# A four-layer graph network on one core: the pair factor of the hyperbolic layers as a degree-4 polynomial, with the old program behind a run-time guard

## The chip, the core and the metric

The kernel runs on one core of one Trainium2 chip. A core has five engines that run their own instruction streams: PE (matrix products, with its weight loads listed as PEld), DVE (VectorE), ACT (ScalarE, activation functions by tables that are loaded as sets), POOL (GpSimd) and SP (SyncE, which issues most DMAs here). SBUF is the on-chip memory with 128 partitions, PSUM the memory that PE writes its products to. The metric is device time in microseconds (us) from one launch of the whole program, the median of several runs. The profile beside it is one execution taken by the hardware profiler.

## What is computed

There are N = 3327 nodes with D = 64 features, and one adjacency matrix `adj` of zeros and ones (density 0.0048). Four layers follow one another. Each takes `h = relu(layernorm(x))` and adds its result to `x`.

```python
h = max(layernorm(x), 0); x = x + L0(h, adj)     # hyperbolic attention
h = max(layernorm(x), 0); x = x + L1(h, adj)     # decayed neighbour sum: w @ (h @ weight) + bias
h = max(layernorm(x), 0); x = x + L2(h, adj)     # signed attention and two GRUs, times the diagonal of adj
h = max(layernorm(x), 0); x = x + L3(h, adj)     # hyperbolic attention with curvature c = 1 / r^2

# L0 and L3
x_t  = logmap0(h)                                 # h * artanh(|h|) / |h|
att  = sigmoid(left(x_t)[:, None] + right(x_t)[None, :] + b) * adj
sup  = sum over j of att[i, j] * logmap(h_i, h_j) # a vector for each pair of nodes
out  = proj(expmap(h, sup))
```

`logmap(h_i, h_j)` holds `artanh(|s|) s / |s|`, where `s` is the Moebius sum of `-h_i` and `h_j`. So each pair of nodes has a direction that is linear in `h_j` and a scalar factor that is not.

## The kernel before

The host pads the nodes to NP = 3328 = 26 x 128, that is by **one** row of zeros in `x`, and one row and one column of zeros in `adj`, which is given transposed (`adjT`). The tile `X` [128, 26, 64] holds all nodes for the whole program; node `t * 128 + p` lies in partition `p`, slot `t`, so the padding row is partition 127 of slot 25. The four layers run one after another: `hyperbolic(att0, ...)`, `decay_sum()`, `signed_gat()`, `hyperbolic(att3, ...)`, and then `X` is written to `out`. Which instruction goes to which engine is written in the code; the order within an engine, buffers and waits are set by the framework's scheduler, except that in the pair loop of `hyperbolic` the order on ACT is kept as written (`manual_schedule`), because tables are switched there by hand.

`hyperbolic` has three parts.

1. A set-up: layer norm and relu into `H`, the squared norms `x2`, the logarithmic map for the attention terms, and transpositions by PE (`to_columns`) into `LdT`, `L2T` and `RT`, whose rows are the 64 features and two more.
2. The pair loop: over 4 chunks of W = 832 target columns and 13 pairs of source blocks of 128 rows. A pair loads 832 KB of `adjT`, makes two sigmoids and multiplies them into `adj` on POOL. For each of the two blocks PE makes `den` (line 274) and `dd` (line 276) in two halves of 416 columns, DVE clips and combines them (277, 278), POOL multiplies (282), ACT takes Ln, Exp and Square (284 to 287), POOL and DVE make a Newton step (288, 289), DVE forms `z` and `v` (292 to 295), ACT takes two logarithms after another table load (303, 304), DVE corrects for rounding (305, 306), POOL adds (307, 308), DVE multiplies up to the weight `w` (309, 311), and PE sums `rows^T w` over the 26 blocks in PSUM (`acc`, 313).
3. An ending on [128, 26, 64] tiles: Moebius algebra on DVE, node by node, and `X += res`.

`decay_sum` and `signed_gat` also go over blocks of `adjT`. In `decay_sum`, the sum comes out transposed, as `outT` [64, NP], and is written for all NP columns by

```python
A.activation(outT[:, c0 + h * BK:c0 + (h + 1) * BK], acc[h], AF.Identity, bias=bias)
```

after which `X` gets `outT` transposed, all 26 slots of it. In `signed_gat`, `X` gets the layer's result times `dcol`, the diagonal of `adjT`.

Of the kernel before, what the change touches and what calls it, by code (L numbers as in the profile page):

```python
# [9 lines left out]
F32 = mybir.dt.float32  # L10
BF = mybir.dt.bfloat16
AF = mybir.ActivationFunctionType
OP = mybir.AluOpType
# [3 lines left out]
N = 3327          # nodes  # L17
P = 128
T = 26            # node tiles
NP = T * P        # nodes, padded with rows and columns of zeros  # L20
D = 64
BK = 416          # columns of one PSUM bank in use; 8 of them make NP
# [4 lines left out]


@with_exitstack
def tile_gnn4(ctx: ExitStack, tc: tile.TileContext, x, adjT, att0, b0, w1, bias1, w_gat, a_gat,  # L30
              wih_e, whh_e, bih_e, bhh_e, wih_n, whh_n, bih_n, bhh_n, r3, att3, b3, out):
    """x [NP, D]; adjT [NP, NP] with adjT[j, i] = adj[i, j]; the GRU weights come as [in, 3D],
    their biases as [D, 3]. Node n = t * P + p lies in partition p, slot t."""
# [18 lines left out]
    tiny_c = column(1e-19, "tiny_c")  # L52

    X = const.tile([P, T, D], F32, name="X")
    nc.sync.dma_start(X, x.rearrange("(t p) d -> p t d", p=P))
# [5 lines left out]
    def wide(t, n=D):  # L61
        """[P, T] -> [P, T, n], the same value along the last dim."""
        return t[:, :, None].to_broadcast([P, T, n])

    def bcast_rows(dram, n=1):
        """A DRAM vector of n values in every partition."""
        return bass.AP(tensor=dram.tensor, offset=dram.offset, ap=[[0, P], [1, n]])

    def sqrt_(pool, src, name):
        """sqrt of a small positive tile: the table's value and one Newton step."""  # L70
        s0 = pool.tile(list(src.shape), F32, name=name)
        rc = pool.tile(list(src.shape), F32, name=name + "_r")
        A.activation(s0, src, AF.Sqrt)
        V.reciprocal(rc, s0)
        V.tensor_mul(rc, rc, src)
        V.tensor_add(s0, s0, rc)
        V.tensor_scalar(s0, s0, 0.5, None, op0=OP.mult)
        return s0

    def norm_relu(pool, h):  # L80
        """h = max(layernorm(X), 0)"""
# [14 lines left out]
    def to_columns(psum, dst, src, rows, post=None):  # L96
        """dst [rows, NP] = src [P, T, rows] transposed"""
# [7 lines left out]
    def to_rows(psum, src, rows, use):  # L105
        """use(t0, n, [P, n, rows]) for src [rows, NP] transposed, some tiles at a time"""
# [9 lines left out]
    def split3(pool, src, name):  # L116
        """fp32 src as the exact sum of three bf16 tiles"""
# [11 lines left out]
    def drop_diagonal(a, b, c0, w):  # L129
        """a [P, w] holds adjT[b*P:, c0:c0+w]: zero what lies on the diagonal"""  # L130
# [4 lines left out]

    def hyperbolic(att, b_att, r, min_norm, min_norm2):
        """X += proj(expmap(h, sum_j sigmoid(left + right) adj logmap(h_i, h_j))).

        In coordinates scaled by sqrt(c) the ball has radius 1. With den = 1 - 2xy + x2 y2 and
        d2 = |x - y|^2, |num|^2 = den d2 holds for num = -(1 - 2xy + y2) x + (1 - x2) y, so that  # L140
        the summand is att artanh(|num|/den) num/|num|. num is linear in (y, y2, 1): the sum over j
        is one product with those rows. The summand of j = i is zero."""
        W = 2 * BK
        with ExitStack() as st:
            pers = st.enter_context(tc.tile_pool(name="hy", bufs=1))
            rows = pers.tile([P, T, D + 2], F32, name="rows")      # [h', x2', 1]
# [9 lines left out]
            lns = pers.tile([P, 1], F32, name="lns")      # brings den d2 into the range of Ln  # L156
# [5 lines left out]
            with tc.tile_pool(name="hyp", bufs=1) as tp, tc.tile_pool(name="hyps", bufs=2, space=PSUM) as ps:  # L162
# [40 lines left out]
                rows2 = tp.tile([P, T, D + 2], F32, name="rows2")  # [h', 1, x2']  # L203
# [4 lines left out]
                # x_t = h artanh(z)/z with z = |h'|; below the floor artanh(z)/z is 1 in fp32  # L208
# [25 lines left out]
                V.tensor_scalar(RT, LdT, sc, None, op0=OP.mult)    # [-2h', x2', 1]  # L234
# [11 lines left out]
            with tc.tile_pool(name="hyadj", bufs=3) as ap, tc.tile_pool(name="hyw", bufs=2) as wk, \  # L246
# [3 lines left out]
                for c in range(NP // W):  # L250
                    c0 = c * W
                    acc = [pa.tile([D + 2, BK], F32, name=f"acc{h}") for h in range(2)]
                    for b2 in range(T // 2):
# [12 lines left out]
                        for s in range(2):  # L266
# [13 lines left out]
                            # y = -2/|num|, by logarithms and one Newton step  # L280
# [9 lines left out]
                            # z = |num|/den, clipped  # L290
# [6 lines left out]
                        A.preload_act_table_set("natural_log")  # the set with the more exact Ln  # L297
                        for s, (y, z, v) in enumerate(pair):
                            b = 2 * b2 + s
                            # lu = 2 artanh(z), with what was rounded off in 1 + z and 1 - z  # L300
# [17 lines left out]
            with tc.tile_pool(name="hye", bufs=1) as tp, tc.tile_pool(name="hyps", bufs=2, space=PSUM) as ps:  # L318
# [3 lines left out]
                m, q, s = M[:, :, :D], M[:, :, D], M[:, :, D + 1]  # L322

                def dot(a, b_, name):
                    prod = tp.tile([P, T, D], F32, name="prod", bufs=2)
                    V.tensor_mul(prod, a, b_)
                    o = tp.tile([P, T], F32, name=name)
                    V.reduce_sum(o, prod, axis=AX.X)
                    return o

                def axpby(a, xx, b_, yy, name):
                    """a x + b y, a and b one value per node"""
                    o = tp.tile([P, T, D], F32, name=name)
                    o2 = tp.tile([P, T, D], F32, name="prod", bufs=2)
                    V.tensor_mul(o, xx, wide(a))
                    V.tensor_mul(o2, yy, wide(b_))
                    V.tensor_add(o, o, o2)
                    return o

                # v = sum_j w (-(1 - 2xy + y2) x + (1 - x2) y)  # L340
                ca = dot(hs, m, "ca")
                V.scalar_tensor_tensor(ca, ca, 2.0, s, op0=OP.mult, op1=OP.subtract)
                V.tensor_sub(ca, ca, q)
                bx = tp.tile([P, T], F32, name="bx")
                V.tensor_scalar(bx, x2, -1.0, 1.0, op0=OP.mult, op1=OP.add)
                vv = axpby(ca, hs, bx, m, "vv")
                f = tp.tile([P, T], F32, name="f")
                V.tensor_scalar(f, bx, MIN_NORM, None, op0=OP.max)
                th = tp.tile([P, T], F32, name="th")
                if r is None:  # L350
                    # expmap of h at the point f v: second = h tanh(t)/(t g), t = |h|/g,
                    # g = max(1 - |f v|^2, MIN_NORM); below 1e-4 tanh(t)/t is 1 in fp32
                    V.tensor_mul(vv, vv, wide(f))
                    p2 = dot(vv, vv, "p2")
                    by = tp.tile([P, T], F32, name="by")
                    V.tensor_scalar(by, p2, -1.0, 1.0, op0=OP.mult, op1=OP.add)
                    g = tp.tile([P, T], F32, name="g")
                    V.tensor_scalar(g, by, MIN_NORM, None, op0=OP.max)
                    V.reciprocal(g, g)
                    t = tp.tile([P, T], F32, name="t")  # L360
                    V.tensor_scalar(t, x2, min_norm2, None, op0=OP.max)
                    t = sqrt_(tp, t, "ts")
                    V.tensor_mul(t, t, g)
                    V.tensor_scalar(t, t, 1e-4, None, op0=OP.max)
                    A.activation(th, t, AF.Tanh)
                    V.reciprocal(t, t)
                    V.tensor_mul(th, th, t)
                    V.tensor_mul(th, th, g)
                    second = tp.tile([P, T, D], F32, name="second")
                    V.tensor_mul(second, hs, wide(th))  # L370
                    point, p2, bp = vv, p2, by
                else:
                    # expmap of f v at the point h': second = v tanh(t)/t, t = max(|v|, min_norm/f)
                    t = dot(vv, vv, "t")
                    V.tensor_scalar(t, t, 1e-8, None, op0=OP.max)
                    t = sqrt_(tp, t, "ts")
                    V.reciprocal(f, f)
                    V.scalar_tensor_tensor(t, f, um, t, op0=OP.mult, op1=OP.max)
                    A.activation(th, t, AF.Tanh)
                    V.reciprocal(t, t)  # L380
                    V.tensor_mul(th, th, t)
                    V.tensor_mul(vv, vv, wide(th))
                    point, second, p2, bp = hs, vv, x2, bx
                # mobius_add(point, second)
                y2 = dot(second, second, "y2")
                xy = dot(point, second, "xy")
                V.tensor_scalar(xy, xy, 2.0, 1.0, op0=OP.mult, op1=OP.add)
                a1 = tp.tile([P, T], F32, name="a1")
                V.tensor_add(a1, xy, y2)
                res = axpby(a1, point, bp, second, "res")  # L390
                V.tensor_mul(y2, y2, p2)
                V.tensor_add(y2, y2, xy)
                V.tensor_scalar(y2, y2, MIN_NORM, None, op0=OP.max)
                V.reciprocal(y2, y2)
                V.tensor_mul(res, res, wide(y2))
                # proj
                n2 = dot(res, res, "n2")
                V.tensor_scalar(n2, n2, maxn2, None, op0=OP.max)
                n2 = sqrt_(tp, n2, "ns")
                V.reciprocal(n2, n2)  # L400
                V.tensor_scalar(n2, n2, 1.0 - 0.004, 1.0, op0=OP.mult, op1=OP.min)
                if isqc is not None:
                    V.tensor_scalar(n2, n2, isqc, None, op0=OP.mult)
# [283 lines left out]
```

## Time and profile before

| what | value |
|---|---|
| median of 3 runs | 4569.69 us (4567.25 to 4571.99) |
| profiled execution: span from first to last instruction | 4563.9 us |
| profiled execution: own time | not listed apart from the span |
| instructions | 22255 |
| PE, PEld, DVE, ACT, POOL busy | 2499.5, 1044.7, 3750.4, 2000.1, 2514.0 us |
| HBM read, written | 178.41 MB, 0.85 MB |
| mean granted TensorE clock | 0.621 of full |
| `X` loaded; last write of `X`; DMA of `out` issued | 0.8 us; 4555.8 us; 4557.7 us |

Lines of a group read: line of the kernel, engine, operation, tile written <- tiles read, shape, how often | busy us in all, mean ns of one | idle time of the engine just before them and what ended it. Rows of a stretch read: start and end, length, and the busy time of PE, PEld, DVE, ACT and POOL with the number of instructions, then the granted clock of PE (1.00 is full), the mean busy share of the 16 DMA engines and GB/s.

### The profile page before, as it was taken

What the parts mean: (1) busy time and instruction counts of PE and PEld (TensorE: products, weight loads), DVE (VectorE), ACT (ScalarE), POOL (GpSimd) and SP (SyncE); (2) the same over time, 40 slices, a digit from 0 to 9 for tenths busy, and PEclk for the clock granted to TensorE, in tenths of its full rate; (3) what the DMA queues carried; (4) which work ended last, traced back from release to release, by engine and by line L of the source; (5) the groups of instructions that cost most, each with busy time, mean ns of one, the idle gap of its engine ahead of it and who ended that gap; (6) DMA issues with size and microseconds to landing.
All of it is one profiled execution on the core that took longest, in us unless ns stands there. A gap on an engine that the chain in (4) does not pass through costs nothing.

```text
span 4563.9 us, 22255 instructions
## 1 busy us (share of the span) xinstructions
PE 2499.5 (55%) x6796; PEld 1044.7 (23%) x6796; DVE 3750.4 (82%) x3373; ACT 2000.1 (44%) x2106; POOL 2514.0 (55%) x1077
## 2 busy tenths in 40 slices
PE   6555455445454452566899686555455544545541
PEld 3111111111111110233576123111111111111110
DVE  6999899989989998654544646999899989989998
ACT  3444444444444443233565224444444454444442
POOL 3676666666666664466000004676666666666672
PEclk7555555555555555799999555555555555555555
DMA  1000000000000000343453000000000000000000
GB/s 38 23 30 23 23 30 23 30 23 30 23 30 23 23 30 0 135 150 105 134 153 107 0 0 30 30 23 30 22 23 30 30 23 22 30 23 22 30 23 8
DMA packets 63144, 180.70 MB, mean 40 GB/s; under 512 B 16112, under 2 KB 16432, under 8 KB 63024
## 3 DMA queue, kind: packets, MB, share of 16 engines
q1 hardware_dynamic: 58544, 179.26, 12.6%
q8 instruction: 53, 0.87, 0.1%
q10 hardware_dynamic: 4480, 0.02, 0.1%
q14 instruction: 67, 0.55, 0.0%
HBM read 178.41 MB, written 0.85 MB: 39 GB/s over the span
## 4 chain that ended last, share of the span: by engine, by line
DVE 67%; PE 14%; POOL 13%; issue 3%; ACT 2%; DMA 0%; POOLq 0%; ACTq 0%; DVEq 0%; SPq 0%
DVE lu L309 12%; DVE v L305 12%; DVE z L292 10%; POOL lu L308 10%; DVE w L311 6%; DVE v L306 6%; DVE y L289 4%; DVE z L293 3%; PE pv L562 3%; DVE dm L277 3%; DVE df L278 2%; POOL S L476 2%; PE pn L559 2%; DVE v L295 2%; PE acc L468 1%
## 5 line engine op out<-in xcount | busy, mean ns | idle before, releaser
L313 PE MATMUL acc<-w,rows 128*66 128x416 f32 x832 | 624.5, 905 | 887.4 <-DVE w L311 887.4
L276 PE MATMUL dd<-RT,L2T 66*128 66x416 f32 x832 | 660.8, 895 | 787.2 <-DVE df L278 787.2
L309 DVE TENSOR_TENSOR lu<-lu,y 128x832 f32<-128x832 f32 x208 | 564.5, 2714 | 219.9 <-POOL lu L308 219.9
L308 POOL TENSOR_TENSOR lu<-lu,v 128x832 f32<-128x832 f32 x208 | 458.1, 2203 | 452.9 <-DVE v L306 452.9
L282 POOL TENSOR_TENSOR p<-dm,df 128x832 f32<-128x832 f32 x208 | 463.5, 2228 | 378.2 <-DVE df L278 378.2
L305 DVE SCALAR_TENSOR_TENSOR v<-z,v 128x832 f32<-128x832 f32 x208 | 635.0, 3053 | 0.0
L307 POOL TENSOR_TENSOR lu<-lu,lv 128x832 f32<-128x832 f32 x208 | 404.7, 1946 | 410.2 <-ACT lv L304 335.0
L288 POOL TENSOR_TENSOR q<-q,p 128x832 f32<-128x832 f32 x208 | 546.0, 2625 | 150.9 <-ACT q L287 150.9
L303 ACT ACTIVATE lu<-z,one_c 128x832 f32<-128x832 f32 x208 | 205.6, 988 | 858.4 <-DVE z L293 858.4
L284 ACT ACTIVATE y<-p,tiny_c,lns 128x832 f32<-128x832 f32 x208 | 224.7, 1080 | 790.9 <-DVE lu L309 774.4
L274 PE MATMUL den<-RT,LdT 66*128 66x416 f32 x832 | 507.3, 738 | 53.7 <-DVE dm L277 52.8
L276 PEld LDWEIGHTS dd<-RT,L2T 66*128 66x128 f32 x832 | 217.2, 303 | 1212.4 <-DVE df L278 1122.7
L292 DVE TENSOR_TENSOR z<-df,y 128x832 f32<-128x832 f32 x208 | 478.0, 2298 | 2.8
L264 POOL TENSOR_TENSOR adj<-adj,sig 128x1664 f32<-128x1664 f32 x104 | 422.0, 4057 | 76.9 <-ACT sig L261 76.8
L313 PEld LDWEIGHTS acc<-w,rows 128*66 128x66 f32 x832 | 158.2, 220 | 1303.6 <-DVE w L311 1062.1
L311 DVE SCALAR_TENSOR_TENSOR w<-lu,adj 128x832 f32<-128x832 f32 x208 | 331.4, 1593 | 0.3
L274 PEld LDWEIGHTS den<-RT,LdT 66*128 66x128 f32 x832 | 226.7, 281 | 335.1 <-issue 189.8
L306 DVE SCALAR_TENSOR_TENSOR v<-z,v 128x832 f32<-128x832 f32 x208 | 294.6, 1416 | 0.0
L278 DVE SCALAR_TENSOR_TENSOR df<-dm,floor,dd 128x416 f32<-128x416 f32 x416 | 264.8, 636 | 6.3 <-PE dd L276 6.3
L562 PE MATMUL pv<-value,H 128*64 128x416 f32 x832 | 268.0, 512 | 0.0
L289 DVE SCALAR_TENSOR_TENSOR y<-q,y 128x832 f32<-128x832 f32 x208 | 211.8, 1018 | 67.6 <-POOL q L288 67.6
L548 DVE TENSOR_SCALAR mask<-adj 128x832 bf16<-128x832 f32 x208 | 124.4, 600 | 155.2 <-PE pc L561 138.6
(300 smaller groups left out, 4284.0 us busy)
## 6 DMA issues: line engine op xcount, KB each, us to landing
adj<-in SPq DMA_DIRECT2D x156, 832.0 KB, 4.5
adj<-in SPq DMA_DIRECT2D x104, 416.0 KB, 3.3
X<-in SPq DMA_DIRECT2D x1, 832.0 KB, 7.7
out<-X SPq DMA_DIRECT2D x1, 832.0 KB, 5.3
wie<-in SPq DMA_DIRECT2D x1, 96.0 KB, 2.1
whe<-in SPq DMA_DIRECT2D x1, 48.0 KB, 2.3
win<-in SPq DMA_DIRECT2D x1, 48.0 KB, 2.3
whn<-in SPq DMA_DIRECT2D x1, 48.0 KB, 2.2
```

What stands on the lines that cost most here:

```text
L264: G.tensor_tensor(adj, adj, sig, op=OP.mult)
L274: PE.matmul(den, LdT[:, b * P:(b + 1) * P], RT[:, cs], start=True, stop=True)
L276: PE.matmul(dd, L2T[:, b * P:(b + 1) * P], RT[:, cs], start=True, stop=True)
L282: G.tensor_tensor(p, dm, df, op=OP.mult)
L288: G.tensor_tensor(q, q, p, op=OP.mult)
L292: V.tensor_mul(z, df, y)
L305: V.scalar_tensor_tensor(v, z, 1.0, v, op0=OP.add, op1=OP.subtract)
L306: V.scalar_tensor_tensor(v, z, 2.0, v, op0=OP.mult, op1=OP.subtract)
L308: G.tensor_tensor(lu, lu, v, op=OP.add)
L309: V.tensor_mul(lu, lu, y)
L311: V.scalar_tensor_tensor(w, lu, -0.25, adj[:, s, :], op0=OP.mult, op1=OP.mult)
L313: PE.matmul(acc[h], rows[:, b, :], w[:, h * BK:(h + 1) * BK], start=(b == 0), stop=(b == T - 1))
```

## The change

Both hyperbolic layers get a new function, `hyperbolic_series`. It takes one product per pair of nodes, L = LT^T RT, and replaces the factor of the pair by a polynomial of degree 4 in L. The polynomial holds for rows whose squared norm `x2` is at least `X2_MIN` = 18, and a guard counts the rows for which that is so. The old four-layer program stands once more at the end of the kernel, inside `tc.If`, and runs when the count is not 2 N. The Moebius algebra of the ending moves into a function `move` that both variants call; comments are dropped throughout.

```diff
+G0, G1, G2, G3, G4 = 0.30970640316, -0.36098355479, 0.46940675477, -1.28660460234, 2.86920527402
+X2_MIN = 18.0
...
+    def hyperbolic_series(att, b_att, r, min_norm, min_norm2, ok):
+        W = 2 * BK
+        R = D + 1
...
+                good = tp.tile([P, T], F32, name="good")
+                V.tensor_scalar(good, x2, X2_MIN, None, op0=OP.is_ge)
+                V.reduce_sum(ok, good, axis=AX.X)
+                V.tensor_scalar(ia, x2, 1.0, None, op0=OP.subtract)
+                V.reciprocal(ia, ia)
+                V.tensor_mul(rows[:, :, :D], hs, wide(ia))
+                V.tensor_scalar(rows[:, :, :D], rows[:, :, :D], 2.0, None, op0=OP.mult)
+                V.scalar_tensor_tensor(rows[:, :, D], x2, 1.0, ia, op0=OP.add, op1=OP.mult)
...
+                to_columns(ps, LT, rows, R)
...
+                V.tensor_scalar(RT, LT, sgn, None, op0=OP.mult)
...
+            with tc.tile_pool(name="hsadj", bufs=4) as ap, tc.tile_pool(name="hsw", bufs=3) as wk, \
+                    tc.tile_pool(name="hsps", bufs=3, space=PSUM) as ps, \
+                    tc.tile_pool(name="hsacc", bufs=1, space=PSUM) as pa:
+                for c in range(NP // W):
+                    c0 = c * W
+                    acc = [pa.tile([R, BK], F32, name=f"acc{h}") for h in range(2)]
+                    for b2 in range(T // 2):
+                        adj = ap.tile([P, 2, W], F32, name="adj")
+                        nc.sync.dma_start(adj, adjT[2 * b2 * P:(2 * b2 + 2) * P, c0:c0 + W]
+                                          .rearrange("(s p) i -> p s i", p=P))
+                        sig = wk.tile([P, 2, W], F32, name="sig")
+                        for s in range(2):
+                            b = 2 * b2 + s
+                            drop_diagonal(adj[:, s, :], b, c0, W)
+                            A.activation(sig[:, s, :], leftB[:, c0:c0 + W], AF.Sigmoid,
+                                         bias=right[:, b:b + 1])
+                        G.tensor_tensor(adj, adj, sig, op=OP.mult)
+                        for s in range(2):
+                            b = 2 * b2 + s
+                            L = ps.tile([P, 2, 512], F32, name="L")
+                            for h in range(2):
+                                PE.matmul(L[:, h, :BK], LT[:, b * P:(b + 1) * P],
+                                          RT[:, c0 + h * BK:c0 + (h + 1) * BK], start=True, stop=True)
+                            Lu = L[:, :, :BK]
+                            y = wk.tile([P, 2, BK], F32, name="y")
+                            A.activation(y, Lu, AF.Square, scale=0.5, bias=g1_c)
+                            y2 = wk.tile([P, 2, BK], F32, name="y2")
+                            A.activation(y2, y, AF.Square, bias=g2_c)
+                            V.scalar_tensor_tensor(Lu, Lu, 0.5 * G3, y2, op0=OP.mult, op1=OP.add)
+                            w = wk.tile([P, 2, BK], F32, name="w")
+                            V.scalar_tensor_tensor(w, Lu, G4 - 0.5 * G3, adj[:, s, :].rearrange(
+                                "p (h i) -> p h i", h=2), op0=OP.add, op1=OP.mult)
+                            for h in range(2):
+                                PE.matmul(acc[h], rows[:, b, :], w[:, h, :],
+                                          start=(b == 0), stop=(b == T - 1))
+                    for h in range(2):
+                        A.activation(accT[:, c0 + h * BK:c0 + (h + 1) * BK], acc[h], AF.Copy)
...
+                V.tensor_scalar(ia, ia, G0, None, op0=OP.mult)
+                sq0 = tp.tile([P, T], F32, name="sq0")
+                V.tensor_mul(sq0, M[:, :, D], ia)
+                V.tensor_scalar(ia, ia, 0.5, None, op0=OP.mult)
+                m = tp.tile([P, T, D], F32, name="m")
+                V.tensor_mul(m, M[:, :, :D], wide(ia))
+                move(tp, hs, x2, m, sq0, None, r, min_norm2, um, maxn2, isqc)
...
-    hyperbolic(att0, b0, None, 1e-15, 1e-30)
-    decay_sum()
-    signed_gat()
-    hyperbolic(att3, b3, r3, math.sqrt(1e-15), 1e-15)
-    nc.sync.dma_start(out.rearrange("(t p) d -> p t d", p=P), X)
+    def load():
+        nc.sync.dma_start(X, x.rearrange("(t p) d -> p t d", p=P))
+
+    def layers(hyp, *more):
+        hyp(att0, b0, None, 1e-15, 1e-30, *more[:1])
+        decay_sum()
+        signed_gat()
+        hyp(att3, b3, r3, math.sqrt(1e-15), 1e-15, *more[1:])
+        nc.sync.dma_start(out.rearrange("(t p) d -> p t d", p=P), X)
+
+    load()
+    ok = const.tile([P, 2], F32, name="ok")
+    layers(hyperbolic_series, ok[:, 0:1], ok[:, 1:2])
+
+    bad = const.tile([1, 1], F32, name="bad")
+    badi = const.tile([1, 1], mybir.dt.int32, name="badi")
+    with tc.tile_pool(name="okps", bufs=1, space=PSUM) as ps:
+        po = ps.tile([1, 2], F32, name="po")
+        PE.matmul(po, one_c, ok, start=True, stop=True)
+        V.reduce_sum(bad, po, axis=AX.X)
+    V.tensor_scalar(bad, bad, 2.0 * N, None, op0=OP.not_equal)
+    V.tensor_copy(badi, bad)
+    with tc.If(nc.values_load(badi, min_val=0, max_val=1,
+                              skip_runtime_bounds_check_because="the outcome of a comparison") > 0):
+        load()
+        layers(hyperbolic)
```

The series loop has no `manual_schedule` and no table preloads of its own. `hyperbolic` in the branch is the old one, line for line.

## The prediction, made before the changed kernel ran

> **What bounds the kernel now.** I read the table of engines first, then the stretches by stage, then the groups. The first says VectorE (DVE) is busy 82% of 4563.9 us, but that is an average over four layers, so I cut the span where one layer's last write to X ends. Columns: length, busy time of PE, PEld, DVE, ACT, POOL, granted clock, DMA share, GB/s.
>
> ```profile
> 0.00:59.50 59.50, 30.90 (x146) 22.18 (x146) 29.45 (x56) 14.26 (x27) 0.70 (x6) 0.91 0.13 15
> 59.50:1785.00 1725.50, 863.36 (x1257) 302.24 (x1258) 1567.95 (x1247) 804.51 (x786) 1151.43 (x496) 0.56 0.08 26
> 1785.00:1838.40 53.40, 3.66 (x18) 1.38 (x16) 48.84 (x60) 5.55 (x8) 1.13 (x2) 0.56 0.00 0
> 1838.40:2174.30 335.90, 212.40 (x1136) 116.59 (x1136) 177.81 (x187) 103.26 (x121) 192.52 (x50) 0.95 0.40 132
> 2174.30:2728.10 553.80, 491.02 (x2820) 276.38 (x2820) 282.27 (x466) 245.47 (x339) 16.80 (x28) 0.79 0.29 81
> 2728.10:2780.00 51.90, 30.80 (x147) 22.19 (x148) 29.44 (x62) 17.35 (x32) 0.00 (x0) 0.63 0.01 1
> 2780.00:4508.00 1728.00, 864.64 (x1260) 302.54 (x1261) 1570.00 (x1248) 804.18 (x786) 1151.47 (x496) 0.56 0.08 26
> 4508.00:4563.90 55.90, 2.73 (x15) 1.14 (x13) 44.63 (x51) 5.55 (x8) 0.00 (x0) 0.53 0.07 16
> ```
>
> The two pair loops (second and seventh line) take 1725.5 + 1728.0 = 3453.5 us; everything else 1110.4. In them DVE is busy 91%. The groups say with what:
>
> ```profile
> L309 DVE TENSOR_TENSOR lu<-lu,y 128x832 f32<-128x832 f32 x208 | 564.5, 2714 | 219.9 <-POOL lu L308 219.9
> L264 POOL TENSOR_TENSOR adj<-adj,sig 128x1664 f32<-128x1664 f32 x104 | 422.0, 4057 | 76.9 <-ACT sig L261 76.8
> L465 DVE SCALAR_TENSOR_TENSOR w<-rk,e 128x832 bf16<-128x832 f32 x104 | 101.3, 1016 | 13.1 <-ACT e L462 13.1
> L462 ACT ACTIVATE e<-rk,ebias 128x832 f32<-128x832 f32 x104 | 93.6, 950 | 195.5 <-PE rk L460 195.5
> L261 ACT ACTIVATE sig<-leftB,right 128x832 f32<-128x832 f32 x208 | 194.3, 981 | 1.2
> L287 ACT ACTIVATE q<-y 128x832 f32<-128x832 f32 x208 | 186.6, 897 | 6.6
> ```
>
> L309 reads two SBUF tiles and lasts 2.7 us on the mean, beside a busy POOL. L465 (decay layer), as wide but with one operand in PSUM, takes 1.0. One pair of row blocks (104 pairs over both layers) costs 3453.5 / 104 = 33.2 us.
>
> **Part 1: the series loop** replaces all of this by a short list. Per pair:
> - ACT: two sigmoids (L261, 0.98 us), two squares from PSUM (as L462, 0.95), two from SBUF (between L287's 0.90 and L261's 0.98): 5.66 to 5.82 us.
> - DVE: four instructions with one PSUM operand, as L465: 4.1 us. POOL: L264 once, 4.06. DMA: 832 KB; the decay layer moved 132 GB/s, which is 6.5 us for that, with the DMA engines busy 0.40, so it has room.
> - PE: an fp32 product is two passes (L313 appears 832 times for 416 in the code). Two blocks with two products for the polynomial and two for the sum make 16 passes. Their spacing has two values, read from the weight loads between neighbours:
>
> ```profile
> 1783.62 0.24 PEld L313 LDWEIGHTS acc<-w,rows 128*66 128x66 f32 x1 [0.46 <-issue]
> 1784.32 0.24 PEld L313 LDWEIGHTS acc<-w,rows 128*66 128x66 f32 x1 [0.46 <-issue]
> ...
> 1788.48 0.14 PEld L313 LDWEIGHTS acc<-w,rows 128*66 128x66 f32 x1 [0.21 <-issue]
> 1788.83 0.14 PEld L313 LDWEIGHTS acc<-w,rows 128*66 128x66 f32 x1 [0.21 <-issue]
> ```
>
> 0.70 us at the low clock, 0.35 at the full one: 11.2 or 5.6 us a pair. Which? Short stretches:
>
> ```profile
> 403.80:407.20 3.40, 3.40 (x6) 1.59 (x5) 3.40 (x4) 0.25 (x1) 1.74 (x1) 0.50 0.62 235
> 407.20:410.60 3.40, 2.56 (x5) 0.87 (x4) 3.40 (x6) 1.89 (x2) 0.73 (x1) 0.50 0.00 0
> 427.70:431.10 3.40, 3.40 (x6) 1.28 (x6) 2.12 (x2) 0.00 (x0) 3.40 (x2) 0.50 0.00 0
> 431.10:434.50 3.40, 1.48 (x4) 0.30 (x2) 3.40 (x3) 2.28 (x3) 2.76 (x2) 1.00 0.00 0
> 2580.00:2728.00 148.00, 142.24 (x214) 37.77 (x214) 56.58 (x99) 30.03 (x49) 0.00 (x0) 0.50 0.00 0
> ```
>
> A full PE alone does not raise the clock: the stretch from 403.8 (mostly passes of 66 rows) and the GRUs from 2580 (three passes of four with 64 rows) stay at 0.50. The one from 427.7 is mostly the four passes of the sum, with 128 rows, and the next is at 1.00. The new loop has both kinds half and half: its four 128-row passes take 2.8 us at the low clock, so that some 3.4 us stretch soon looks like that from 427.7. Falling back took an emptier PE: the stretch from 431.1 was busy 1.48 of 3.4. With PE at 85 to 95% the full clock should last; I take 5.6.
>
> The Trainium skill, "TensorE: Matmul & The Clock Gate", Part 1, has the array at half rate until about 3.4 us of sustained activity release it. By that rule PE is at full clock here; but the GRUs' 148 us at 0.50 do not agree with it, so rows and not the rule decide.
>
> PE (5.6) and ACT (5.7) stand level, DVE and POOL at 4. How near to them does such a loop come? The signed layer's loop (products x832 from 2195.2 to 2487.5 us, 104 blocks) takes 2.81 us a block, which is its PE time: nothing lost. The decay loop (1877.7 to 2170.4, 52 steps) takes 5.6 where its largest engine, POOL, is busy 4.0: 40% over, since each step is a chain through four engines. The new loop is a chain too (product 1.4, squares 1.9, two DVE instructions 2.0, sum 1.4) but has three PSUM buffers for it: 5.3 / 3 = 1.8 us per block against 2.85 needed. I take 12% over 5.7, nearer to the first: 6.4 us a pair. Per layer 52 x 6.4 + 6 to fill and drain = 339 us in place of 1726. Ends: 5.6 (294) and 8.0 (422); 11.2 is a rival.
>
> **Part 2: around the loop.** The set-up loses the transposition of the second factor (7 ACT copies of 0.56 us alternating with PE, some 5 us) and a 1.0 us copy; it gains a wide multiply (1.9), a wide scaling (1.0), four small instructions of 0.2 to 0.3. The ending gains one wide multiply (1.9) and 0.4. Net zero within 5 us a layer. First pass: 1110 + 2 x 339 = 1788 us.
>
> **Part 3: the guard, and what it decides.** `ok` counts in each hyperbolic layer the rows with x2 >= 18 over all 26 x 128 = 3328 rows, the padding row among them; the branch is skipped only if both counts add up to 2 x 3327 = 6654. From the reference's inputs (layer norm, relu, sum of squares), the smallest x2 of a true node is 23.86 in the first layer and 23.50 in the last: all count, 6654. The padding row is zero in the first layer, x2 = 0, not counted. But the decay layer ends with an activation that adds the bias to every column of outT, the padding's too, and X += that. From there on the padding row of X is the bias vector; its diagonal entry is 0, so the signed layer adds nothing. In the last layer it is normalised like any row: worked out from the bias given, x2 = 30.47. It counts. The sum is 6655, `not_equal` gives 1, and **the general path runs as well**: load, four layers, out written again.
>
> So none of the old program is saved; all of it is appended. The second pass is before's 4563.9 us less the 0.8 us ahead of its X load: 4563. Its transfers and first instructions wait on every queue behind the branch, so nothing of it overlaps the first pass.
>
> The guard itself: a two-pass product (0.3 us each), four small DVE instructions (0.2), a value read by the engines, and their meeting at the branch; the last two have no row. Below, 1.5 us by the chain alone; above, 25, five landings as slow as w_l's 4.9. I take 10, towards the low end, since a register read moves less. A gain is excluded: it comes on top.
>
> The Trainium skill, "Runtime: NRT & Kernel Launch", Instruction fetch mechanics, speaks against a branch: one taken to a target outside the fetched window stalls for a fetch. No run here shows it.
>
> **Sum.** 1788 + 10 + 4563 = 6361 us of span. No separate time is listed for the profiled execution; the median of the runs, 4569.7, is 5.8 above the span. So 6367 us.
>
> **Rivals.**
> - *The guard holds.* If the padding row's x2 in the last layer were below 18, or not a number, the count would be 6654 and the branch skipped: 1788 + 10 + 6 = 1804 us, faster. The sign hangs on this one row. Against: 30.47 is far from 18, and the bias reaches the padding by an instruction that spans all columns. 0.06.
> - *General path taken, series loop slower than its engines.* PE held at the low clock: 11.2 us a pair, 104 x 4.8 = 500 us more, 6867. Squares and sigmoids in different tables, two loads of 1.28 us a pair: ACT 8.3, 200 more, 6567. The decay loop's 40%: 166 more, 6533. Against the tables: L287's squares followed exponentials without a load. 0.19.
> - *As forecast.* 0.75.
>
> **Numbers.** Range 6255 to 6600: from 5.6 us a pair, 7 us less around each loop and a guard of 2 (1110 + 588 - 14 + 2 + 4563 + 6) to beyond the table case with the guard's 25. Left out: the skipped branch (0.06) and the low clock (0.1). A measurement of this kernel can tell some 0.2% from no change. Slower by more 0.93; faster 0.06; within it 0.01, as no case lies there.
>
> **What would show it.** Right: the old pair loop's groups (x208, three table loads x104) still in the page, from about 1800 us on; two writes of out; 181 MB grown to about 361; in the first pass's pair loops PE and ACT near 90%, clock above 0.85. Wrong: no rows of the general path; a first pass beyond 1950 us, which puts the error in the 6.4; or a second pass not within 15 of 4563.

## The result, and the profile after

The changed kernel takes 6415.6 us (median of 4 runs, 6407.4 to 6423.1) against 4569.4 us before (4567.3 to 4572.0): 1.404 times as long, 95% interval 1.402 to 1.406. The forecast was 6367. The branch was taken, so the program computes the four layers twice; the new pair loops alone are 63 us longer than forecast, and the other terms give some 15 us back, which leaves the 49 us that the forecast falls short.

The page of the changed kernel: its span, and in 40 slices of 160 us the granted clock and the DMA rate.

```profile
span 6409.9 us, 38893 instructions
...
PEclk8988999659965555555555589996555555555555
...
HBM read 356.81 MB, written 1.70 MB: 56 GB/s over the span
```

The clock row has the four layers of the series program in its first 11 or 12 digits, and then the clock of the old program, 5 in its long loops. Bytes are twice those of before, 178.41 and 0.85 MB.

Next, the value that decides the branch (tile `badi`): who reads it, and from when on; then DMAs issued from 1836 to 1847 us, with KB and us to landing; then the timeline there.

```profile
L829 DVE CAST badi<-bad x1: 134/134/134, 1791.2 to 1791.2; 1x1 int32<-1x1 f32 x1
L830 POOLq TENSOR_LOAD <-badi x1: 497/497/497, 1791.3 to 1791.3; - x1
L830 SPq TENSOR_LOAD <-badi x1: 597/597/597, 1837.0 to 1837.0; - x1
```

```profile
out<-X SPq DMA_DIRECT2D x1, 832.0 KB, 4.9
X<-in SPq DMA_DIRECT2D x1, 832.0 KB, 5.0
bcol<-in ACTq DMA_DIRECT2D x1, 0.5 KB, 2.9
```

```profile
1836.57 0.39 SPq L815 DMA_DIRECT2D out<-X  x1
...
1841.52 0.37 SPq L808 DMA_DIRECT2D X<-in  x1
```

The count was ready at 1791.3 us, 45 us before the first pass was over: its product and the three small DVE instructions behind it lie inside the ending, and so do the reads by POOL and PE. Only SP's read, 0.6 us, comes behind the issue of `out`. `X` is loaded again at 1841.52 us, just when `out` has landed (1836.57 + 4.9 = 1841.5); it could not be earlier, since `out` is read from `X`. On this path guard and branch thus cost nothing beside what lies there anyway.

The span by stage (columns as in the prediction). Set-up, series loop, ending; decay layer; signed layer; set-up, series loop, ending; landing of `out`; second pass.

```profile
0.00:53.50 53.50, 24.07 (x120) 18.87 (x120) 31.40 (x60) 10.77 (x20) 0.70 (x6) 0.93 0.11 17
53.50:420.00 366.50, 322.43 (x828) 139.48 (x828) 211.00 (x209) 285.56 (x319) 204.83 (x80) 0.92 0.38 121
420.00:473.60 53.60, 4.04 (x32) 2.41 (x30) 49.78 (x61) 5.55 (x8) 0.29 (x1) 0.57 0.00 0
473.60:810.00 336.40, 213.95 (x1136) 117.12 (x1136) 177.00 (x182) 103.20 (x121) 192.13 (x50) 0.94 0.40 132
810.00:1364.50 554.50, 488.51 (x2820) 276.01 (x2820) 284.01 (x470) 245.44 (x339) 17.87 (x28) 0.80 0.29 81
1364.50:1411.00 46.50, 25.10 (x113) 19.16 (x113) 30.67 (x62) 11.03 (x21) 0.00 (x0) 0.61 0.01 1
1411.00:1785.60 374.60, 326.54 (x842) 142.56 (x842) 211.97 (x209) 285.59 (x320) 204.85 (x80) 0.92 0.37 119
1785.60:1836.50 50.90, 2.26 (x29) 1.86 (x27) 47.08 (x56) 5.04 (x7) 0.00 (x0) 0.54 0.00 0
1836.50:1841.50 5.00, 0.00 (x0) 0.00 (x0) 0.30 (x10) 0.00 (x0) 0.00 (x0) 0.50 0.76 171
1841.50:6409.90 4568.40, 2498.57 (x6796) 1043.53 (x6796) 3752.98 (x3360) 1998.61 (x2105) 2514.49 (x1071) 0.62 0.13 40
```

The last row is the whole old kernel: VectorE busy 3753 us where it was 3750. The two series loops take 366.5 + 374.6 = 741.1 us in place of 3453.5. They are 7.05 and 7.20 us a pair, where the forecast had 339 / 52 = 6.52 with its filling. PE is busy 88% of them and ACT 77%: neither is full, so each waits for a part of the time. The groups of the series loop (first pass, both layers):

```profile
L348 POOL TENSOR_TENSOR adj<-adj,sig 128x1664 f32<-128x1664 f32 x104 | 386.5, 3717 | 233.4 <-DMA adj<-in 185.3 <-ACT sig L346 12.3 <-ACT y L357 11.5
L365 PE MATMUL acc<-w,rows 128*65 128x416 f32 x832 | 360.0, 559 | 92.0 <-DVE w L362 87.8 <-ACT accT L368 3.3
L360 DVE SCALAR_TENSOR_TENSOR L<-L,y 128x832 f32<-128x832 f32 x208 | 214.0, 1031 | 296.9 <-ACT y L359 296.8
L362 DVE SCALAR_TENSOR_TENSOR w<-L,adj 128x832 f32<-128x832 f32 x208 | 212.7, 1024 | 17.9 <-POOL adj L348 3.5 <-DVE L L360 0.9
L359 ACT ACTIVATE y<-y,g_c 128x832 f32<-128x832 f32 x208 | 203.7, 981 | 2.6
L346 ACT ACTIVATE sig<-leftB,right 128x832 f32<-128x832 f32 x208 | 202.0, 981 | 96.1 <-POOL adj L348 95.8
L357 ACT ACTIVATE y<-L,g_c 128x832 f32<-128x832 f32 x208 | 195.6, 941 | 61.6 <-PE L L353 61.2
```

Durations are as forecast, but for POOL: 1.03 and 1.02 us for the DVE instructions with an operand in PSUM, 0.94 to 0.98 on ACT (5.80 us a pair, added up), 3.72 on POOL, where the prediction had 4.06. The waits form a ring: POOL's product waits for its load, ACT's sigmoid for POOL's product, PE for `w`, DVE for ACT. What ACT itself waited for in the first of the two loops (60 to 420 us; waiter, releaser: us, times, longest):

```profile
ACT sig L346 <- POOL adj L348: 46.5, 33, 3.4
ACT y L357 <- PE L L353: 28.8, 20, 3.9
ACT accT L368 <- PE acc L365: 2.5, 4, 1.1
```

These make 78 of the 81 us in which ACT is idle in that loop (366.5 less 285.6).

### The profile page after: what moved, and what is told of

Read it like the earlier page. It is cut to its first block, busy times and chain, and to the rows that moved or that the text cites. A ratio compares the mean times of both kernels' runs of the same rounds, so it can differ in the third digit from the quotient of the medians.

```text
span 6409.9 us, 38893 instructions
## 1 busy us (share of the span) xinstructions
PE 3905.5 (61%) x12710; PEld 1761.0 (27%) x12710; DVE 4796.2 (75%) x4673; ACT 2950.8 (46%) x3260; POOL 3135.2 (49%) x1316
## 5 line engine op out<-in xcount | busy, mean ns | idle before, releaser
L550 DVE SCALAR_TENSOR_TENSOR v<-z,v 128x832 f32<-128x832 f32 x208 | 635.1, 3053 | 0.0
L138 POOL TENSOR_TENSOR adj<-adj,offdiag 128x128 f32<-128x128 f32 (+1 forms) x168 | 87.7, 534 | 1067.0 <-DMA adj<-in 1030.9
L724 PE MATMUL pv<-value,H 128*64 128x416 f32 x1664 | 537.5, 514 | 0.0
L348 POOL TENSOR_TENSOR adj<-adj,sig 128x1664 f32<-128x1664 f32 x104 | 386.5, 3717 | 233.4 <-DMA adj<-in 185.3
L710 DVE TENSOR_SCALAR mask<-adj 128x832 bf16<-128x832 f32 x416 | 249.4, 601 | 311.2 <-PE pc L723 278.9
L721 PE MATMUL pn<-mask,h 128*64 128x416 bf16 x2496 | 466.0, 340 | 0.9 <-ACT hT L107 0.9
L638 POOL TENSOR_TENSOR S<-S,mask 128x1664 bf16<-128x1664 bf16 x96 | 377.7, 3934 | 181.8 <-PE rk L622 163.1
L509 POOL TENSOR_TENSOR adj<-adj,sig 128x1664 f32<-128x1664 f32 x104 | 422.3, 4061 | 81.0 <-ACT sig L506 80.9
L713 ACT ACTIVATE value<-adj 128x832 f32<-128x832 f32 x416 | 351.0, 889 | 219.0 <-issue 209.9
```

Source lines behind the costliest of these rows:

```text
L550: V.scalar_tensor_tensor(v, z, 1.0, v, op0=OP.add, op1=OP.subtract)
L638: G.tensor_tensor(S2, S, mask, op=OP.add)
L721: PE.matmul(pn[h][o, :], parts[i][:, b, :], masks[k][:, cs], start=first and i == 0, stop=last and i == 2)
L724: PE.matmul(pv[h][o, :], H[:, b, :], values[k][:, cs], start=first, stop=last)
```

## The experiments

Two questions. Is it the padding row that opens the branch, as the prediction has it? And why does a pair take 7.1 us where the instructions of its largest engine add up to 5.8? For the second the candidates were the four buffers of `adj`, since POOL's product waits longest for loads (e3); the three sigmoid tiles (e4); the order of the instructions on ACT, which the scheduler sets (e6, e7); and the turns from one chunk to the next, where the sum must be finished and copied (e8). Whether the clock follows the rows is asked by e5. Letters in the expectations stand for the theories that they name. All have the padding row taken out of the count, or no guard, so that the first pass stands alone.

**e1: the padding row is not counted.** `offdiag` is zero on the diagonal, and its last column is therefore 1 for partitions 0 to 126 and 0 for 127.

```diff
                 V.tensor_scalar(good, x2, X2_MIN, None, op0=OP.is_ge)
+                V.tensor_mul(good[:, T - 1:T], good[:, T - 1:T], offdiag[:, P - 1:P])
                 V.reduce_sum(ok, good, axis=AX.X)
```

> The changed kernel with the padding row taken out of the count (its entry of good is multiplied by 0). If the padding row alone makes the count 6655, the count is now 6654, the branch is skipped and the time is the first pass: about 1837 us to the issue of out plus 5 to 12, so 1842 to 1855 us. If the count is off for another reason (a true row below 18, or a value that is not a number), the general path still runs and the time stays at 6416 us.

Measured: 1842.6 us (1834.4 to 1850.2), 0.403 of before (0.4015 to 0.4047). With one row less in the count the branch is not taken and 4573 us are gone. That the padding row alone opens it is shown.

**e2: no guard and no branch.** Everything behind `layers(hyperbolic_series, ...)` is deleted.

> The series layers alone: no final count, no branch, no general path (the rows are still counted, the counts are not read). Against e1_pad_out it prices the guard when it holds. If the value read and the branch only follow the last DMA, as the 5 us from out to the next X load say, it is 0 to 8 us faster than e1_pad_out. If a skipped branch costs a stall of the engines as well, 10 to 25 us faster.

Measured: 1837.9 us (1828.5 to 1840.8), 0.402 (0.4004 to 0.4033). e1 is 4.7 us longer, with overlapping ranges. In the traces `out` is issued 1833.45 us into e1, whose span is 1840.9, and 1828.38 us into e2, whose span is 1833.7: 7.4 and 5.3 us to the end. So a branch that is skipped costs some 2 us behind the last transfer, and the other 5 us are ahead of it, in pair loops with the same code. The Trainium skill, "Runtime: NRT & Kernel Launch", Instruction fetch mechanics, warns of a fetch stall for a branch out of the fetched window; if one is in these 2 us, which two traces show, it is no larger than that.

**e3: six buffers for `adj`**, on top of e1.

```diff
-            with tc.tile_pool(name="hsadj", bufs=4) as ap, tc.tile_pool(name="hsw", bufs=3) as wk, \
+            with tc.tile_pool(name="hsadj", bufs=6) as ap, tc.tile_pool(name="hsw", bufs=3) as wk, \
```

> e1_pad_out with six adj buffers in the series loop in place of four. Theory A, the ring of adj buffers sets the pair's 7.1 us (SP waits for DVE's w 321 us in one layer, POOL waits for the landing, ACT for POOL, DVE for ACT): a pair falls to 6.0 to 6.4 us, 104 x 0.7 to 1.1 = 75 to 115 us less than e1_pad_out. Theory B, the ring of sigmoid tiles or the order of the ACT queue sets it: within 10 us of e1_pad_out.

Measured: 1923.3 us (1918.5 to 1928.2), 0.421 (0.4202 to 0.4221): 81 us longer than e1. More room made it slower, which neither theory had. The edit gives the scheduler another order to choose, too; in e3's waits from 60 to 430 us one is new among the first:

```profile
DVE L L361 <- ACT y L360: 185.0, 71, 9.6
...
ACT y L358 <- PE L L354: 87.5, 29, 7.2
```

ACT's first square waits 87.5 us for a product, where the changed kernel had 28.8 in 60 to 420 us. The clock in the loop fell to 0.87 (0.92). So more buffers alone mend nothing, and the order comes under suspicion. That four buffers are enough is shown only by e9, which keeps them.

**e4: six sigmoid tiles**, on top of e1.

```diff
-                        sig = wk.tile([P, 2, W], F32, name="sig")
+                        sig = wk.tile([P, 2, W], F32, name="sig", bufs=6)
```

> e1_pad_out with six sigmoid buffers in place of three, adj still four. Theory A (adj ring): within 15 us of e1_pad_out, since POOL still waits for the landing. Theory B (sigmoid tiles: ACT waited 96 us for POOL's read of them in both layers): 60 to 95 us less.

Measured: 1822.4 us (1820.2 to 1829.5), 0.399 (0.3983 to 0.4002), 20 us less than e1, short of the 60 to 95 of its theory. It is a part, and a small one.

**e5: all products of the pair loop with 64 or 65 rows**, on top of e2. The sum takes the first 64 of each block's 128 source rows; half of it is left out.

```diff
-                                PE.matmul(acc[h], rows[:, b, :], w[:, h, :],
+                                PE.matmul(acc[h], rows[:D, b, :], w[:D, h, :],
```

> e2_no_guard with the products of the sum over 64 of the 128 rows only (half of each block's sum is left out). Same number of passes and columns, but now all products of the pair loop have 64 or 65 rows. If the clock follows rows times busy time, as the passes of 66 rows and the GRUs at 0.50 suggest, the pair loops run at 0.50, PE needs 11.2 us a pair, and the time is e2_no_guard plus 104 x (11.2 - 7.1) = about 430 us, some 2260. If sustained activity alone releases the clock, it stays above 0.9 and the time within 15 us of e2_no_guard.

Measured: 2359.8 us (2356.1 to 2363.5, two runs), 0.5165 (0.5153 to 0.5176): 522 us longer than e2, with the same number of instructions and less to compute. The row of its loop:

```profile
60.00:400.00 340.00, 337.93 (x452) 109.47 (x450) 116.57 (x114) 166.57 (x185) 124.12 (x46) 0.50 0.24 78
```

PE is busy 99% of 340 us, at a clock of 0.50. In the changed kernel, where half of the passes have 128 rows, PE is busy 88% at 0.92. So the rows count, as the prediction argued from two short stretches and the GRUs, and a busy PE alone is not enough. Half of the passes is no rule by itself either: in the GRUs of the kernel before, two passes of 128 rows alternate with two of 64 for 9.4 us at a time, at a clock of 0.50.

```profile
2594.45 1.65 PE L618 MATMUL pr<-ns,wie 128*64 128x416 f32 x2
2596.03 1.65 PE L619 MATMUL pr<-hT,whe 64*64 64x416 f32 x2
```

The new loop has mostly four of each in a row; that this makes the difference is the prediction's argument, and no run varies it alone. e5 also halves rows times columns of the changed passes (64 x 65 for 128 x 65). That it is rows and not this product rests on the prediction's stretch from 403.8 us alone, with 66 x 128 at 0.50, and so on 3.4 us. The rule of the Trainium skill, "TensorE: Matmul & The Clock Gate", Part 1, that about 3.4 us of sustained activity release the clock, is not what this row shows.

**e6: ACT in the order written**, on top of e1.

```diff
-                    tc.tile_pool(name="hsacc", bufs=1, space=PSUM) as pa:
+                    tc.tile_pool(name="hsacc", bufs=1, space=PSUM) as pa, \
+                    tc.manual_schedule(engines={mybir.EngineType.Activation}):
```

> e1_pad_out with the order on ACT kept as written in the series loop (two sigmoids, then two squares for each of the two blocks, pair after pair) in place of the scheduler's, which puts sigmoids of later pairs among the squares. Theory C, a sigmoid that waits for a buffer or a landing holds the squares queued behind it on ACT, and through them DVE and PE: ACT comes near to its 5.7 us a pair, 6.0 to 6.3, so 85 to 115 us less than e1_pad_out, about 1740. Theory A (the four adj buffers): no gain, within 15 us, or a loss as sigmoids come later and POOL's 3.7 us stands ahead of each first w.

Measured: 1879.7 us (1878.5 to 1881.2), 0.411 (0.4108 to 0.4121), 37 us longer. As written, a pair's sigmoids stand right before its squares, and POOL's 3.7 us product lies between them and the first `w`. Its waits from 60 to 400 us show it:

```profile
POOL adj L350 <- ACT sig L348: 141.9, 41, 8.9
```

The scheduler's order was the better one of these two; whether a third order on ACT would mend the loop, this run does not say. Theory C's gain of 85 to 115 us did not come; a loss through POOL's product ahead of each first `w` had been named beside theory A.

**e7: load, sigmoids and POOL's product one pair ahead**, on top of e6; `attention` holds these three.

```diff
+                adj = attention(*pairs[0])
+                for n, (c, b2) in enumerate(pairs):
...
+                    following = attention(*pairs[n + 1]) if n + 1 < len(pairs) else None
                     for s in range(2):
...
+                    adj = following
```

> e6_as_written with the load, sigmoids and POOL product of each pair written one pair ahead of its squares, order on ACT kept. Theory C: POOL's product is off the chain, ACT and PE bound at 5.7 us, 5.7 to 5.9 us a pair: 125 to 145 us less than e1_pad_out, about 1710, and 10 to 40 less than e6_as_written. Theory A: with one pair more held in the same four adj buffers it is slower than e6_as_written.

Measured: 1816.2 us (1814.9 to 1817.0), 0.397 (0.3968 to 0.3981): 26 us less than e1, where theory C had 125 to 145, and 64 less than e6, where theory A had a loss: four `adj` buffers hold one pair more without harm. Its trace is now regular, and shows the two losses that are left. First stretches of it, a steady one and one across a chunk's turn:

```profile
71.00:143.00 72.00, 67.20 (x186) 29.33 (x184) 44.13 (x44) 61.74 (x68) 44.22 (x13) 1.00 0.41 132
143.00:166.00 23.00, 17.20 (x41) 7.19 (x40) 10.13 (x11) 13.79 (x17) 9.45 (x7) 0.85 0.27 90
```

Then ACT's timeline at the turn, and further on (in brackets the wait, and what ended it):

```profile
142.35 0.99 ACT L369 ACTIVATE y<-y,g_c 128x832 f32<-128x832 f32 x1
146.77 0.51 ACT L379 ACTIVATE accT<-acc 65x416 f32<-65x416 f32 x1 [3.44 <-PE acc L375]
...
200.04 0.95 ACT L367 ACTIVATE y<-L,g_c 128x832 f32<-128x832 f32 x1 [1.22 <-PE L L363]
```

At a turn the copy of the finished sum stands in ACT's queue ahead of the next sigmoids and squares; ACT waits 3.44 us for PE, PE's next sums then wait 4.4 us for a `w` that those squares delay, and the clock drops to 0.85 on the mean of that stretch. Between turns ACT waits 1.22 us in every second pair for a product: PE had it queued behind a sum that itself waited for `w`.

**e8: the copy of the sum on DVE**, on top of e7.

```diff
-                            A.activation(accT[:, c0 + h * BK:c0 + (h + 1) * BK], acc[h], AF.Copy)
+                            V.tensor_copy(accT[:, c0 + h * BK:c0 + (h + 1) * BK], acc[h])
```

> e7_sig_ahead with the two copies of acc at the end of a chunk of columns made by DVE in place of ACT. In e7 a chunk takes 88 us although pairs in its middle come every 6.15 us: at each turn ACT waits 3.4 us for the last sum, its squares of the next chunk come late, and the clock falls to 0.50 for 7 to 10 us. If the turn is what is lost, each of the 8 turns gives back 4 to 7 us: 1816 less 30 to 55, some 1775. If the loss is in the order of PE's queue instead, within 12 us of e7.

Measured: 1769.1 us (1768.4 to 1770.0), 0.387 (0.3864 to 0.3877): 47 us less, over 8 turns 5.9 us each; of this at most 8 us can be the 16 copies of 0.51 us themselves, of which ACT is rid. In e7's order the turns were the largest loss found so far.

**e9: PE in a fixed order too**, on top of e8: the product of block n + 2 stands ahead of the sum of block n.

```diff
+                    if n + 2 < len(blocks):
+                        ready.append(product(*blocks[n + 2]))
                     for h in range(2):
                         PE.matmul(acc[h], rows[:, b, :], w[:, h, :],
                                   start=(b == 0), stop=(b == T - 1))
```

> e8_turn_dve with PE's order written out as well: the two products of block n + 2 always ahead of the sum of block n. In e7 the scheduler's PE order leaves half of a product behind a sum that waits for DVE, and ACT idles 1.2 us for it once in two pairs (pairs of 5.5 and 6.8 us in turn). If that is what is left, every pair takes 5.5 to 5.7 us, 104 x 0.55 = 55 us less than e8_turn_dve. If the three PSUM buffers or POOL's product set the pair, no gain, within 12 us.

Measured: 1707.5 us (1706.9 to 1708.7), 0.374 of before (0.3730 to 0.3743): another 62 us. The first pair loop of e1, e7, e8 and e9, one row from each, and of e9 a steady stretch of ten pairs:

```profile
53.50:422.70 369.20, 329.13 (x842) 143.33 (x843) 212.31 (x209) 285.26 (x320) 204.77 (x80) 0.92 0.37 120
```

```profile
53.50:411.90 358.40, 322.96 (x843) 140.39 (x843) 211.54 (x209) 289.38 (x320) 204.58 (x80) 0.93 0.38 124
```

```profile
53.50:387.90 334.40, 310.61 (x843) 135.96 (x843) 214.79 (x216) 286.04 (x313) 204.76 (x80) 0.97 0.41 133
```

```profile
53.50:356.80 303.30, 300.06 (x845) 139.78 (x846) 212.70 (x216) 288.86 (x313) 204.86 (x80) 0.97 0.46 147
74.00:130.00 56.00, 56.00 (x161) 26.06 (x160) 40.18 (x41) 55.34 (x61) 38.32 (x12) 1.00 0.49 153
```

The steps of the loop, -10.8, -24.0 and -31.1 us, are about half of each step of the whole, as two layers should have it. In the last row PE is busy throughout, ACT 99%, at the full clock: ten pairs in 56 us, the 5.6 us that the prediction read from the spacing of the passes. ACT's six durations add up to 5.8, but in the trace neighbours overlap by up to 0.1 us (a sigmoid pair from 73.39 us lasts 1.85 us, and the next square starts at 75.14). e9 is also the version to keep: it guards the true rows alone, still holds the general path, and beats before and the changed kernel.

## Why the prediction was right, and where it was 49 us off

- **The branch is taken.** Right, and for the reason given: the decay layer writes the bias into the padding row, which then counts in the last layer. e1 takes that row out, and the branch is skipped.
- **The second pass.** 4563 forecast, 4568.4 measured (+5). "Nothing of it overlaps the first pass" holds but for a trifle: its load of `X` follows the landing of `out`, while some small memsets and the 0.5 KB load of `bcol` start from 1836.6 us on, under that landing.
- **The guard.** 10 us forecast, within 1.5 to 25; nothing measured on the path where the branch is taken, below the lower bound, and some 2 us where it is skipped. What was wrong here put the count's arithmetic behind the end of the first pass. The last layer's `x2` is known at its set-up, and so the count and two of the reads were done 45 us earlier. The stop at the branch is covered by the landing of `out`, which the 1788 already held.
- **Around the loops.** "Net zero within 5 us a layer": 53.5 + 53.6 + 46.5 + 55.9 = 209.5 against 220.7 before, 11 us less, 5.6 a layer and so just outside; the two other layers are 1 us longer.
- **The series loops.** The term that was mis-sized: 6.4 us a pair and 6 to fill, 678 for both layers, against 741.1 (+63). With -10 around the loops, -10 for the guard and +5 for the second pass that makes the 49 of the span (6409.9 against 6361), to rounding. The sign "PE and ACT near 90%" held for PE (88%), not for ACT (77%). The low end of the range has a slip: its 294 us for 5.6 us a pair leave 3 us to fill where the 339 have 6; that moves the end by 6 us and decides nothing.
- **Why 6.4 was too little.** The engines' own times were right or on the safe side: PE 5.6, ACT 5.8 added up, DVE 4.1, POOL 3.7. The 12% were an interpolation between a loop that loses nothing and one that loses 40%, and three buffers for the products were said to cover the chain. They cover its length, not the order of the queues. With the same three buffers, four `adj` and three sigmoid tiles, and the same work (one copy moves from ACT to DVE), e9 takes 135 us less than e1, in three steps: a pair's head start for sigmoids and POOL 26, the turns of the chunks 47, PE's order 62. ACT's idle time in the first loop falls from 81 us in the changed kernel to 14 (303.3 less 288.9).
- **What these steps do not say of the changed kernel.** They are prices in the orders in which they were tried, and the turns are the clearest case. In the changed kernel, whose order on ACT is the scheduler's, the first `w` of the second chunk follows the last one of the first after 2.07 us, ahead of the copies, which start without a wait:

```profile
157.79 1.02 DVE L362 SCALAR_TENSOR_TENSOR w<-L,adj 128x832 f32<-128x832 f32 x1
159.86 1.02 DVE L362 SCALAR_TENSOR_TENSOR w<-L,adj 128x832 f32<-128x832 f32 x1
161.93 0.90 ACT L368 ACTIVATE accT<-acc 65x416 f32<-65x416 f32 x2
```

Going by the starts of `w`, twelve blocks across a turn of this loop (it has three inside) take 4 to 5 us less than twelve in the middle of the chunk before; in e7 they take 7 to 8 us more, in e8 as long to within 0.3 us. Inside its four chunks the changed kernel takes 6.4 to 7.6 us a pair, where the middle of e7's chunks has 6.2 and of e9's 5.6. So e7's order gained inside the chunks and lost a part again at the turns; the changed kernel lost its 63 us inside the chunks, where ACT waits for POOL to be done with a sigmoid tile and for products.

- **The clock.** "With PE at 85 to 95% the full clock should last": 88% and 0.92 measured. The rival with the low clock had 11.2 us a pair, 500 us more than at 6.4. e5 shows that it would have cost more: 12.0 us a pair (452 passes in 340 us, 16 to a pair), 522 us over e2 where 430 were expected.
- **The rivals.** A guard that holds was put at 1804 us; e1 has 1842.6, longer by the same pair term. Table loads are out: the series loop has two in all, one a layer.

```profile
L346 ACT ACT_TABLE_LOAD x2 | 2.6, 1283 | 28.8 <-issue 28.8
```

What stays open is how much of the changed kernel's own loss each of the three steps would mend alone; they were tried one on top of the other. Nor was it followed why the scheduler's order differs so much between four and six buffers.

## What to carry to other kernels

A guard that counts rows must count the same rows as the constant beside it: work out what padding holds at that point, layer by layer, since a bias or a norm fills it. A fallback that is appended costs its whole time when it is taken and next to nothing when it is not, so the condition is the first thing to evaluate on real inputs. Once a loop's engines stand level (here PE and ACT, at 5.6 us a pair), the order in the queues decides: give each producer a step's head start, put a product that is ready ahead of a sum that waits, and where the order is fixed by hand, keep a copy that waits for the end of a sum off the engine that must start the next one. A written order is of use only if it is the right one: e6 was 37 us slower than the scheduler's.

## What was not expected of the hardware

PE stayed at a clock of 0.50 through 340 us of 99% activity, with 64 and 65 rows in every pass (e5). With 128 rows in half of the passes the loop ran at 0.92 (changed kernel), and at 1.00 in e9's steady stretch. So e5, which computes less, takes 2.36 ms against e2's 1.84 ms. A register read of the guard's value took 0.47 to 0.60 us on each engine.
